# Two graph convolution products of neighbouring batches taken together, with seven products of halves in place of eight

## The chip, the cores and the metric

The kernel runs on one core of a Trainium2 chip. The core has five engines that take their instructions in order, each from a queue of its own: TensorE (PE in the profile; it multiplies matrices and sums into PSUM), VectorE (DVE), ScalarE (ACT), GpSimd (POOL) and SyncE (SP, which here issues nearly all transfers). They meet through semaphores. Matrices lie in SBUF as 128 partitions with so many elements each; larger data lie in DRAM. The metric is the device time of one execution in microseconds (us); lower is better.

## The reference, cut to what matters

`x` has 16 batches of 1024 nodes with 256 channels, `adj` is 1024 x 1024, all float32. Two layers follow each other; the change concerns the second.

```python
# layer 0
c   = mean(x, channels)                                  # one number for each node
A_s = likeness of the nodes by c[m] - c[n]               # 1024 x 1024 for each batch
g   = relu((x^T @ (adj * A_s)) * para)                   # becomes the queries q
k, v = split(x @ kv_w)                                   # 4 heads of 64
x   = layernorm(x + softmax(q k^T * scale) @ v)
# layer 1
h   = relu(x @ w1_loop + adj @ (x @ w1_neigh) + b1)      # 1024 x 128, "first convolution"
h   = relu(h @ w2_loop + adj @ (h @ w2_neigh) + b2)      # 1024 x 256, "second convolution"
x   = layernorm(x + (x + h) * 0.5)
```

The two products concerned are `adj @ t1`, with `t1 = x @ w1_neigh` (1024 x 128), and `adj @ h1`, with `h1` the result of the first convolution (1024 x 128; `w2_neigh` is applied after the product). Both have the same left matrix for every batch, and inner and outer sizes of 1024, 1024 and 128.

## The kernel before, in words

**Staging.** The 16 batches go through a pipeline in which three things share the engines. While the attention of batch b runs, the queries of batch b+1 are formed, and layer 1 of batch b-1 is computed. The order of instructions is written by hand (`run`, from L690, under a manual schedule), so each engine executes its part of the program text in that order. SP issues the transfers in the same order, and a transfer that must wait holds those behind it.

**The attention of a batch.** It has four units (`UNITS`), a pair of heads with half of the query nodes each. `att.scores(u)` (L465 to L486) multiplies keys and queries on TensorE (L473), takes exponentials on ScalarE (L476), sums them on VectorE (L482) and turns the sum (L484). `att.outputs(u)` (L488 to L497) multiplies with the values (L493) and turns the result (L497). `att.add(u)` (L499 to L516) forms the denominators with a small product on TensorE (L505, `den_ps`) and adds the outcome into the residual on VectorE (L509 onwards). Between the units run three functions of `run`:

- `first` (L740): loads x of batch b+1 in blocks; `conv.first` of batch b-1 (L580 to L602): t1 (L585, copied by ScalarE at L588), then for each half of 512 nodes two matmuls with `w1l_sb` (L597) and eight with the adjacency (L599) into the same bank, and the relu on ScalarE (L600). Then `turn_blocks` (L604 to L613): h1 is turned in 32 x 32 blocks on VectorE (L608), stored to DRAM and read back node by node, in two halves. Beside that the moments and the normalization of batch b-2 (`old.moments`, `old.finish`), `prepare` (L202: x of batch b+1 turned to channel-major, and partial sums), `att.add(0)` and `means` (L218).
- `second` (L753): begins the queries of b+1 (`q.left` on GpSimd L387 to L392, `q.likeness`, `q.pair(0)`), then `conv.second` of batch b-1 (`neighbours`, L630 to L637: 2 x 8 matmuls with the adjacency, L635, and copies on ScalarE, L637), then `att.add(1)`.
- `last` (L763): `conv.last` of batch b-1 (L652: `outer` L639 to L643 on TensorE, `residual` L645 to L650 on VectorE), then `att.add(2)`.

After the fourth unit come the other query products (L430), the last `att.add(3)`, the keys (`k_ps`, L307), the values (`v_ps`, L319) and the layer norm of batch b in blocks (`BlockedNorm`, L257 to L297), whose `spread` (L288) writes the result node by node to DRAM and reads it back as `x1`.

**Queries.** `FastQueries` (L367 to L450) already multiplies by halves with seven products in place of eight; its combinations are formed by `left` (GpSimd) and `right` (VectorE).

**Batches at the ends.** In batch 0 the adjacency, read in blocks, is turned on VectorE (`turn_adj`, L718 to L720) into `adjT_sb` (L160), which holds all of it as eight tiles of 128 x 1024 for the rest of the run. Batch 1 is the first with a convolution, that of batch 0. In the last batch there are no queries to form, and the convolution of batch 14 is spread over its end; that of batch 15 follows alone (`conv.first`, `conv.second`, `conv.ending`).

**Buffers.** `row_tile` gives a tile of 128 x 1024 from a ring of `ROWS` = 21 (L69). PSUM has three tiles of 128 x 1024 ("big", two banks of 512 each; `half_psum` takes the first half of one) and two single banks. x has three buffers. The transfer of `x1d` and `h1d` goes through DRAM tiles with two buffers each.

The product of the first convolution is

```python
ph = half_psum(f"h1_ps_{b}_{j}")
for cc in range(NC):
    nc.tensor.matmul(ph, w1l_sb[:, cc, :], xT[:, cc, ts(j, FB)], start=(cc == 0), stop=False)
for mt in range(NT):
    nc.tensor.matmul(ph, t1[:, mt, :], adjT_sb[:, mt, ts(j, FB)], start=False, stop=(mt == NT - 1))
nc.scalar.activation(self.h1T[:, ts(j, FB)], ph, AF.Relu, bias=b1_sb)
```

## Time and profile before

| | |
|---|---|
| time, three runs | 2251.86, 2253.75, 2254.12 us, median 2253.75 |
| the profiled execution | 2252.83 us, its span 2251.1 us, mean granted clock of TensorE 0.998 |
| busy: PE, DVE, ACT, POOL | 99%, 79%, 42%, 8% of the span |
| transfers | 189.39 MB, mean 84 GB/s |
| matmuls h_ps (L599) and u_ps (L635) | 512 records each, 224.9 and 224.5 us busy |
| from the first scores of one batch to those of the next | 138.4 us (the starts are at 154.46, 292.91 and 431.34 for the batches 1, 2 and 3) |

The profile comes from one execution. Its page gives busy time by engine, then the chain of work that ended last, followed back from the end; its shares say which engine's work, or which wait, that chain passes through. A group of instructions has its line, its engine, what it writes and reads, how often it occurs, its busy time and the mean of one in ns, and the idle time of the engine just before it with the engine that ended it ("<-"). In a timeline, each row is one or several adjacent instructions with start and length in us; what stands in brackets is how long the engine had been idle, and who released it. A float32 matmul leaves two records, so 512 records of L599 are 256 matmuls.

## The change

For an adjacency in blocks of 512 x 512, a product of it with one matrix of 1024 x 128 takes four products of blocks, and two matrices (t1 of batch c1 = b-1 and h1 of batch c2 = b-2) take eight. The changed kernel forms both results from seven. t1 and h1, each cut in two halves of 512 nodes, make a 2 x 2 matrix of halves; four sums and differences of them are formed for each pair of batches (`left`), four combinations of the adjacency's blocks once for the whole run (`adj_sums`), and the seven products are put together partly by letting them add up in the same PSUM bank and partly with additions.

- **Adjacency.** `adjT_sb` is gone. Three blocks stay in SBUF (`half_adj` 00, 10 and 11). The fourth (01) and the four combinations (1, 2, 3, 4) are in DRAM; every joint product reads the four combinations into row tiles (`fetch`, 2 x 512 KB each, issued by SP). They are formed in batch 1 by `adj_sums`: eight VectorE subtractions of 128 x 1024, and stores. `turn_adj` turns halves of 512.
- **Joint product.** `Joined.left` is four additions or subtractions on GpSimd (on VectorE in the last joint product). `Joined.run` issues the products 1, 2, 6, 7, 5, 4, 3 with four matmuls of 128 x 512 each, the matmuls with `w1l_sb` (`loop`) ahead of 2 and 3, copies to SBUF on ScalarE, two additions on VectorE and one on GpSimd; at set points between them (`between`) it calls other work. `first` and `third` in it are the two halves of one PSUM tile.
- **Scaling.** `w1l_sb` and `w1n_sb` are multiplied by `LIFT` = 32 at the start, and the relu of the first convolution by 1/32.
- **Pipeline.** The second convolution of a batch now comes one batch later than its first, and its normalization another one later, so that three convolutions are under way (`c1`, `c2`, `c3`). `x1` is read back from DRAM when it is needed (`load_x`) instead of at once; `x1d` has three DRAM buffers.
- **Order.** `gap0` (where `first` was): loads, t1 (`inner`), `att.add(0)`, the fetches 2 and 3, `left`, `prepare`. `means` stands after the second scores. `gap1` (where `second` was): `q.left`, `q.likeness`, the fetches 1 and 4, the joint product, and within it `att.add(1)`, the moments of c3, `q.times_adj`, `q.right(0)` and `finish` of c3. In batch 1, where there is no c2, it runs `c1.first` alone and then `adj_sums`. `gap2`: `last` of c2, `turn_blocks` of c1 with one transpose of 128 x 1024, stores to DRAM (read back at the start of the next batch), `att.add(2)`.
- **Ends.** In the last batch the joint product of batches 14 and 13 runs among the steps of the norm; after it come the joint product of 15 and 14, and the second convolution of 15 alone. `ROWS` is 23.

```diff
-    ROWS = 21
+    ROWS = 23
...
-    adjT_sb = const.tile([P, NT, N], F32, name="adjT_sb")
+    half_adj = {(0, 0): const.tile([P, TJ, FB], F32, name="adjT_00"),
+                (1, 0): const.tile([P, TJ, FB], F32, name="adjT_10"),
+                (1, 1): const.tile([P, TJ, FB], F32, name="adjT_11")}
+    far_adj = {n: dram.tile([2, P, N], F32, tag=f"adj_{n}", name=f"adjT_{n}", bufs=1) for n in ("01", 1, 2, 3, 4)}
...
+    def adj_sums(rows01):
...
+            nc.vector.tensor_sub(v[1], w12, w11)
+            nc.vector.tensor_sub(v[3], w22, w12)
+            nc.vector.tensor_sub(v[2], w22, v[1])
+            nc.vector.tensor_sub(v[4], w21, v[2])
...
-        def turn_blocks(self, j):
+        def turn_blocks(self):
+            h1B = row_tile(f"h1B_{self.b}")
+            nc.vector.transpose(h1B, self.h1T)
...
+    class Joined:
...
+        def left(self, eng):
...
+            eng.tensor_add(s12[:, 0], h1[0], h1[1])
+            eng.tensor_sub(s34[:, 0], t1[0], h1[0])
+            eng.tensor_sub(s12[:, 1], s12[:, 0], t1[0])
+            eng.tensor_sub(s34[:, 1], t1[1], s12[:, 1])
...
+        def run(self, between=None):
...
+            ac = big_psum(f"hu_ps_{b}_0")
+            first, third = ac[:, 0:FB], ac[:, FB:N]
+            second = half_psum(f"hu_ps_{b}_1")
...
+            self.product(1, first, start=True)
+            nc.scalar.copy(p1, first)
+            turn_to(1)
+            c1.loop(third, 0, start=True)
+            self.product(2, third)
+            nc.vector.tensor_add(p1, p1, third)
+            turn_to(2)
+            self.product(6, first, again=True)
+            nc.scalar.copy(u1, first)
+            c1.relu(0, p1)
+            turn_to(6)
+            self.product(7, second, start=True)
+            nc.scalar.copy(p7, second)
+            turn_to(7)
+            self.product(5, first, again=True)
+            nc.scalar.copy(u3, first)
+            turn_to(5)
+            self.product(4, second, again=True)
+            c2.uT = row_tile(f"uT_{c2.b}")
+            nc.vector.tensor_add(c2.uT[:, 0:FB], u1, second)
+            nc.gpsimd.tensor_add(c2.uT[:, FB:N], u3, p7)
+            turn_to(4)
+            c1.loop(first, 1, again=True)
+            self.product(3, first, again=True)
+            c1.relu(1, first)
...
+            def gap0():
                 blocked = load_blocked(b + 1, str(b + 1))
...
+                c1.inner()
+                att.add(0)
+                if both:
+                    c2.load_x()
+                    both.fetch(2, 3)
+                    both.left(nc.gpsimd)
                 ready["xT"], ready["part"] = prepare(blocked, str(b + 1))
...
+                if both:
+                    both.fetch(1, 4)
+                    both.run({1: (lambda: q.left(nc.gpsimd), lambda: q.likeness(0)),
+                              2: (lambda: att.add(1),),
+                              6: (lambda: q.likeness(TJ), c3.moments if c3 else lambda: None),
+                              7: (weigh_first,),
+                              5: (lambda: c3 and c3.finish(out[b - 3]),)})
+                else:
...
+                    c1.first(rows01)
+                    att.add(1)
+                    weigh_first()
+                    store("01", rows01)
+                    adj_sums(rows01)
...
+            def gap2():
+                if both:
+                    c2.last()
+                c1.turn_blocks()
+                att.add(2)
...
+                if u == 1 and between:
+                    ready["mean"] = means(ready["part"], str(b + 1))
```

## What is predicted

> **What bounds the kernel now.** I read the page's busy shares first, then its chain of waits, then one steady batch engine by engine in order of time. The page names the bound:

> ```profile
> PE 2230.0 (99%) x8310; PEld 1067.2 (47%) x8310; DVE 1773.9 (79%) x2377; ACT 945.4 (42%) x1026; POOL 187.6 (8%) x104
> ...
> PE 98%; DVE 1%; DMA 0%; ACT 0%; issue 0%; SPq 0%; POOLq 0%; DVEq 0%; POOL 0%; ACTq 0%
> ```

> TensorE is on the chain for 98% of the span, so instructions taken from it are time gained, and every microsecond that it is newly made to wait is lost. VectorE's 79% is an average and has to be read by stage. In the timeline of TensorE (start, length, then what) the two products of a batch are

> ```profile
> 1004.57 7.03 PE L599 MATMUL h_ps<-adjT_sb,t 128*128 128x512 f32 x16
> 1011.44 1.88 PE L597 MATMUL h_ps<-x1T,w1l_sb 128*128 128x512 f32 x4
> ...
> 1034.79 14.00 PE L635 MATMUL u_ps<-adjT_sb,h 128*128 128x512 f32 x32
> 1048.63 0.30 PE L505 MATMUL den_ps<-den_part,fold 128*128 128x32 f32 x2
> 1048.86 7.14 PE L473 MATMUL s<-qT,kT 64*128 64x512 f32 x32
> ```

> A float32 product leaves two records. From start to start, 8 products of L599 take 6.87 us, 0.859 each; 16 of L635 take 13.84, 0.865 each.

> Where TensorE meets VectorE is at the end of the attention:

> ```profile
> 1070.16 1.23 DVE L647 TENSOR_TENSOR z<-h_ps,b_sb 128x1024 f32<-128x1024 f32 x1 [0.97 <-PE h_ps L643]
> 1071.42 1.23 DVE L650 SCALAR_TENSOR_TENSOR x<-z,x 128x1024 f32<-128x1024 f32 x1
> 1072.56 0.52 DVE L509 RECIPROCAL rden<-den_ps 64x16 f32<-64x16 f32 x2
> ...
> 1089.66 0.71 DVE L497 STREAM_TRANSPOSE o<-av 128x512 f32<-128x512 f32 x1
> ```
> ```profile
> 1089.53 1.02 PE L430 MATMUL g_ps<-T,x 128*128 128x512 f32 x2
> 1090.43 0.41 PE L505 MATMUL den_ps<-den_part,fold 128*128 128x32 f32 x2
> ```

> After the wait of 0.97 VectorE has no gap until the transpose at 1089.66. The fourth denominator (`den_ps`) waits for that transpose, which reads the bank it needs; it starts at 1090.43 instead of 1084.28 + 7 x 0.859 = 1090.29. So TensorE already loses 0.14 us there: from the second half of `last` on, VectorE is as critical as TensorE.

> [...] ScalarE begins 0.20 us after the next product starts (2214.79, then 2214.99), and when that next product must wait for ScalarE it restarts 0.06 after it:

> ```profile
> 2214.99 0.69 ACT L600 ACTIVATE h1T<-h_ps,b_sb 128x512 f32<-128x512 f32 x1 [7.84 <-PE h_ps L599]
> ```
> ```profile
> 2215.74 0.66 PE L620 MATMUL h1n_ps<-ident,h1T 128*128 128x128 f32 x4 [0.34 <-ACT h1T L600]
> ```

> [...]

> **The change part by part.** *Removed.* There are 15 joint products, for batches 1 to 15. Each has 7 x 4 matmuls in place of 8 + 8 of each kind: 16 x 0.859 + 16 x 0.865 - 28 x 0.859 = 3.53 us, 52.9 in all. The h product of batch 0 and the u product of batch 15 stay as they were.

> *Hand-offs inside the joint product.* `first` and `third` are halves of one PSUM tile. In the changed kernel's instructions the first `loop` matmul (into `third`) waits for ScalarE's copy of `first`, and product 6 (into `first`) for VectorE's addition of `third`. All of TensorE's queue stands behind each. Copy: 0.20 + 0.59 (the L637 row) + 0.06 = 0.85, and I take 0.88 for the 0.06 to 0.14 of restart. Addition: 0.20 + 0.69 (L441) + 0.06 = 0.95 less the denominator of about 0.2 that lies between = 0.75. The other copies lie beside a whole product (3.44 us) and cost nothing; product 5 and 4 wait for copies finished 2 us before.

> *`turn_blocks` moved.* Two 512-wide transposes (0.71) left a stage where VectorE idled; one of 1024 (1.25, as L484) now stands between L650 and L509 above. Nothing before the transpose `o` can absorb it, as z waits for TensorE: the denominator is late by 1.25 more. `att.add(1)`, the moments and `finish` move into the joint product, where VectorE is to be free by some 58 us into the batch and the scores start at 62: nothing.

> *The mean.* It now stands behind the second scores. Counted from the batch's first scores, `den_ps` 0 comes at 17.8; VectorE's `add(0)` (2.9, as from 1048.97) ends at 20.95 and `prepare` (4.45, as from 1013.00) at 25.4. TensorE is there at 25.1 to 25.2: 0.3. The blocks of x must have landed by 22; before they landed at 24.1, behind two loads of 1 MB, of which one is now behind them and 0.5 MB takes its place: about 21.5. Bounds 0 and 2.

> *POOL.* Four more operations of 1.265 (the L389 row) run at 19 to 23, beside the two two-input operations of `add(0)`. Between 0 (VectorE goes first) and 1.3 (it waits once), and the delayed accumulation may push the addition of `third` by up to 1 more. I take 0.2.

> *DMA.* Four matrices of 1 MB per joint product, 63 MB on 187. The SP queue issues fetches 2 and 3 behind the blocks of x, 1 and 4 behind `q.load`: landing by about 34 and 46, needed at 42 and 49. Hidden inside batches. Row tiles: 8 more in use with 2 more and others freed early; their waits in the instruction list fall on work done before. POOL's scaling of weights and the stores: hidden by 100 us of attention.

> *Batch 1, where no second convolution exists.* TensorE has 20.8 us less there (moved to the end), but VectorE gets 8 subtractions of 1024 (1.22, L268), 9.8 us, in front of the third accumulation. In the batch's time: h product 33 to 50, `add(1)` to 53, weights to 58, sums to 68, accumulation and part 11.7 to 79.8. TensorE is through `av` at 64.4, and its next instruction, the third denominator, waits: 15.4. [...] I take 17.2; both ends 12 (if the sums wait for nothing and the clock holds) and 20.

> *The two joint products at the end.* The copy of t1 is not hidden: 0.20 + 1.01 (L588) + 0.06 = 1.27 each. Hand-offs about 1.4 each, as denominator and folds lie inside them. In the last one, fetch 2 is issued behind the output of batch 12, itself behind `finish`: eight 512 KB loads at 1.75 to 2.2 us, first wanted some 3.5 us before it lands. 3 to 7, I take 4. Together 9.4.

> *The adjacency turned in halves.* Four transposes of 1024 took 4.61 us (L720, from 123.77); eight of 512, 0.64 apart, take 5.1, ahead of the weighting (L349) for which TensorE waited 1.14 us: 0.5 once.

> *Sum* against the profile's own span: 2251.1 - 52.9 + 13 x (0.88 + 0.75 + 1.25 + 0.3 + 0.2 = 3.38) + 17.2 + 9.4 + 0.5 = 2269.2, that is +18.1. The median of the three other runs is 2253.75, 2.65 above that span (the time of the profiled execution itself is 2252.83): 2271.9.

> **Rivals.** *VectorE keeps pace.* Then `den_ps`, the mean and batch 1 don't wait: 13 x 1.75 + 17.2 = 40 less, 2231. For it: VectorE loses `add(1)` from the stretch before the third accumulation, and it is 79% busy overall. Against it: that accumulation starts when the exponentials allow, not when VectorE is free (1052.01 after scores at 1048.86), and the 0.14 above. It decides if VectorE's waits come to under 22 us of these 40: then the kernel isn't slower.

> *The whole saving arrives*: 2253.75 - 52.9 = 2201, if the hand-offs are hidden too. Both waits are in the instruction list, so this is unlikely.

> [...] and about 0.7 more at the addition or the landing of x: 26 more, 2297. For it: four POOL operations beside two-input work in each batch. Against: DMA has room, 38.6% busy on q1.

> *It does not do what it says.* The instruction list has 28 matmuls and 4 of `loop` in each joint product; I leave this at nothing.

> **How the numbers follow.** Forecast 0.58, VectorE keeps pace 0.18, whole saving 0.04, [...] 0.20. Unknown costs alone make the forecast 2255 to 2285 (mean 0 to 2 over 13 batches is the widest, taken by half; batch 1 from -5 to +3; the last fetch -1 to +3). Range 2240 to 2297: it leaves out the faster half of the second case and the third. No change means within 0.2%, 4.5 us, about what a measurement of this kernel can tell. Slower: 0.52 of the forecast and 0.20, so 0.73 with 0.01 of the second; same 0.09, the forecast's low end and the second's high end; faster 0.18.

> **What would show it.** In the profile after: 60 x 2 fewer records of the two products and TensorE's busy share well under 99%; idle before `loop` of about 0.7 to 0.9 a time, at product 6 0.7, at `den_ps` about 1.3 a batch on the transpose `o`; one idle of 12 to 17 us in the second batch; batches of 138.3 instead of 138.45 us (scores at 154.46 and 292.91). Wrong if batches take under 136.5, or if the second batch has no such idle.

## The result and the profile after

The changed kernel takes 2291.32 us (median of 4 runs, 2289.91 to 2295.66) against 2253.34 before: a ratio of 1.0173, 95% interval 1.0155 to 1.019. That is 38.0 us slower, where 18.1 were forecast. The sign was right and the range holds the time, but the change is 2.1 times as large as forecast.

The page of the changed kernel, its busy shares and the chain that ended last:

```profile
PE 2201.1 (96%) x8190; PEld 1046.9 (46%) x8190; DVE 1852.9 (81%) x2413; ACT 964.4 (42%) x1056; POOL 326.0 (14%) x177
...
PE 69%; DVE 17%; SPq 4%; issue 4%; ACT 3%; DMA 3%; POOL 0%; DVEq 0%; POOLq 0%; ACTq 0%
```

TensorE has the 120 records less that were foreseen (8310, now 8190), and it now waits: 96% busy instead of 99%, and the chain leaves it for VectorE in 17% of the span. What it waits for is in the view of its waits (line and tile that waited, who ended it: us in total, times, longest):

```profile
PE mean_ps L256 <- DVE part L249: 14.7, 26, 1.0
PE den_ps L545 <- DVE o L537: 14.6, 13, 1.1
PE hu_ps L769 <- issue: 10.4, 14, 0.8
PE hu_ps L636 <- ACT snap L786: 10.0, 15, 0.7
PE den_ps L545 <- DVE den_part L526: 6.1, 1, 6.1
PE s L513 <- ACT pr L516: 5.7, 2, 3.8
...
PE hu_ps L769 <- DMA adj<-adjT: 3.3, 1, 3.3
PE hu_ps L769 <- ACT t L632: 2.2, 2, 1.1
```

Rows two to four are the fourth denominator, product 6 and the `loop` matmul, each where the prediction put it. The first row, the mean, is the largest and was forecast as one of the smallest. Rows five and six are batch 1, the last two the ending. In a steady batch (one of the 13 from batch 2 to batch 14) TensorE's timeline shows them one after the other:

```profile
726.60 7.14 PE L513 MATMUL s<-qT,kT 64*128 64x512 f32 x32
733.98 0.41 PE L256 MATMUL mean_ps<-part,fold 128*128 128x32 f32 x2 [0.24 <-DVE part L249]
735.11 0.41 PE L256 MATMUL mean_ps<-part,fold 128*128 128x32 f32 x2 [0.72 <-DVE part L249]
735.45 7.09 PE L533 MATMUL av<-pr,v 128*64 128x512 f32 x32
742.47 3.70 PE L769 MATMUL hu_ps<-adjT,t 128*128 128x512 f32 x8
746.84 1.98 PE L636 MATMUL hu_ps<-x1T,w1l_sb 128*128 128x512 f32 x4 [0.68 <-ACT snap L786]
...
752.10 0.30 PE L545 MATMUL den_ps<-den_part,fold 128*128 128x32 f32 x2
753.16 10.54 PE L769 MATMUL hu_ps<-adj,R 128*128 128x512 f32 x24 [0.76 <-issue]
...
812.88 1.02 PE L470 MATMUL g_ps<-T,x 128*128 128x512 f32 x2
815.03 0.41 PE L545 MATMUL den_ps<-den_part,fold 128*128 128x32 f32 x2 [1.13 <-DVE o L537]
```

The number in brackets is only the idle time that the records leave: the first record behind a wait starts that much after the end of the one before it. The price of a wait is better read from start to start, less the pitch of 0.859 for a matmul: 746.84 - 742.47 - 4 x 0.859 = 0.93 for the copy; 753.16 - 752.10 less 0.2 for the denominator = 0.86 for the addition; 815.03 - 812.88 - 0.86 = 1.29 for the fourth denominator; and 1.33 for the mean (735.45 - 726.60 less the 7.06 that the scores take, which is 1.79, less some 0.46 that its four thin matmuls took before, where nothing waited). The label "issue" at product 6 is no cause: VectorE's addition ends at 753.06, 0.10 before it.

Where the 37.0 us between the two profiled spans (2251.1 and 2288.1) lie is seen from the first scores of each batch:

| stretch | before | after | difference | forecast |
|---|---|---|---|---|
| up to batch 1 | 154.46 | 154.83 | +0.4 | +0.5 |
| batch 1 | 138.45 | 135.18 | -3.3 | -3.6 (+17.2, less 20.8 moved to the end) |
| each steady batch (2 to 14) | 138.44 | 139.53 | +1.09 | -0.15 |
| 13 of them | | | +14.2 | -2 |
| more in the late ones among them | | 0.2, 0.7, 2.2, 0.7 | +3.8 | 0 |
| from batch 15 on | 158.4 | 180.3 | +21.9 | +23.1 (20.8 - 7.1 + 9.4) |

Batch 1 and the ending came out within 1.3 us. The 13 steady batches were to gain 2 and lost 18.

## Experiments

Each experiment edits the changed kernel, and the gains are told against its 2291.32 us. The kernel before, run again beside each group of experiments, took 2252.5 to 2253.5 us, so a difference between groups is good to about 1 us.

The first question is why the mean is late. VectorE's timeline in the same batch, with the like instruction of batch 1, where `left` does not run, as first line:

```profile
174.41 0.69 DVE L555 TENSOR_TENSOR xB_a<-xB_a,o 128x512 f32<-128x512 f32 x1
...
727.47 0.68 DVE L553 TENSOR_TENSOR o<-o,rden 128x512 f32<-128x512 f32 x1
728.19 1.64 DVE L555 TENSOR_TENSOR xB_a<-xB_a,o 128x512 f32<-128x512 f32 x1
729.86 0.69 DVE L556 TENSOR_REDUCE sums<-xB_a 128x16 f32<-128x512 f32 x1
730.47 2.36 DVE L216 STREAM_TRANSPOSE xT<-xB 128x1024 f32<-128x1024 f32 x2
732.75 2.30 DVE L249 TENSOR_REDUCE part<-xB 128x32 f32<-128x1024 f32 x2
```

And GpSimd's:

```profile
727.65 1.63 POOL L760 TENSOR_TENSOR R<-t,h 128x512 f32<-128x512 f32 x1 [2.19 <-ACT t L632]
729.24 1.73 POOL L761 TENSOR_TENSOR R<-R,t 128x512 f32<-128x512 f32 x1
731.04 1.28 POOL L762 TENSOR_TENSOR R<-t,R 128x512 f32<-128x512 f32 x1
```

The addition in `att.add(0)` (L555) takes 1.64 instead of 0.69. Of its 64 instances in the run exactly 13 are long, one in each steady batch. The trace shows a chain of operations with two inputs on the two engines. L760 on GpSimd ends 1.13 us after VectorE's multiplication L553 (at 728.15), VectorE's L555 ends 0.55 after L760 (at 729.28), and L761 ends 1.14 after L555 (at 729.83). Each needs after the other's end what it takes alone (1.27, 0.69 and 1.27), less 0.13 to 0.14, as if it had waited for that end. Beside VectorE's operations with one input nothing of the kind is seen in these lines: L556 takes its 0.69 beside L761, and L762 its 1.28 beside the transposes. What makes the two wait for each other is not shown. Against this reading of the late mean stands another: the mean is late because x comes late behind larger transfers.

### The meeting with `left`, or the transfers

`left` without three of its operations:

```diff
-            eng.tensor_sub(s34[:, 0], t1[0], h1[0])
-            eng.tensor_sub(s12[:, 1], s12[:, 0], t1[0])
-            eng.tensor_sub(s34[:, 1], t1[1], s12[:, 1])
-            self.x = {1: t1[0], 2: t1[1], 3: s34[:, 1], 4: h1[1], 5: s12[:, 0], 6: s12[:, 1], 7: s34[:, 0]}
+            self.x = {1: t1[0], 2: t1[1], 3: s12[:, 0], 4: h1[1], 5: s12[:, 0], 6: s12[:, 0], 7: s12[:, 0]}
```

> Of the four operations of left on GpSimd only the first is issued; the products 3, 6 and 7 read its result in place of theirs, so this leaves out three of the four combinations (the number and size of the matmuls stay). Theory A[...]: in the changed kernel the second operation of left (1.63 us) and the two-input addition of add(0) on VectorE (L555, 1.64 instead of 0.69 us) exclude each other, and everything behind it on VectorE, the mean included, is late by 0.95. Without these operations L555 is back at 0.69, the two waits of mean_ps fall from 0.96 to about 0.1 to 0.3 us in a steady batch, and the kernel gains about 0.9 x 10 to 0.95 x 13, that is 9 to 12 us: about 2280. Theory B, the transfers: the mean is late because the blocks of x land late behind and beside the fetched matrices; then L555 may be short, but the transposes of x wait for a DMA instead, and the time stays within 2 us of 2291.

Measured: 2323.49 us (2319.31 to 2334.49), 32 slower. The run decides for both theories in part. L555 takes 0.69 in all 64 instances, as theory A says. But the mean's wait falls only from 14.7 to 6.9, some 0.5 a batch where A expected 0.1 to 0.3, and the transposes of x now wait for their transfer, as theory B says. VectorE's waits for it, in the changed kernel and then here:

```profile
DVE xT L216 <- DMA xB<-in_x_dram: 1.6, 3, 0.6
```
```profile
DVE xT L216 <- DMA xB<-in_x_dram: 5.1, 9, 0.9
```

The late addition had hidden most of a late landing. The time got longer, against both theories, because a far larger wait came up. TensorE's waits, then ScalarE's and VectorE's timeline in one batch, and the like instruction of the changed kernel (the numbers of lines behind `left` are smaller by 3 in this run):

```profile
PE hu_ps L636 <- ACT snap L783: 35.5, 15, 2.6
```
```profile
754.69 0.59 ACT L783 COPY snap<-hu_ps 128x512 f32<-128x512 f32 x1 [12.38 <-DVE accB L524]
```
```profile
742.82 10.50 DVE L522 TENSOR_TENSOR acc<-acc,pr 128x1024 f32<-128x1024 f32 x6
```
```profile
736.29 9.63 DVE L522 TENSOR_TENSOR acc<-acc,pr 128x1024 f32<-128x1024 f32 x6
```

GpSimd runs the four operations of `q.left` in one piece into VectorE's second accumulation, which takes 10.50 for six additions (9.63 in the changed kernel with two of the four beside it, 7.87 without company). And ScalarE's copy of `first` waits for the transpose `accB` to end; in the changed kernel it starts at 746.21, while `accB` runs until 747.21. Probably it gets another row tile of the ring, which is not shown. So the `loop` matmul waits up to 2.6 instead of 0.7, and in 8 of the 13 steady batches the clock falls to half for 3.4 us behind this wait (the granted clock of the whole run was 0.988, in the changed kernel 0.994). Taking work away moved the rest of GpSimd's queue to a worse place: the run shows that the collision makes L555 long, and it does not show its price in time.

The second try leaves nothing out. It shifts `left` to a time at which VectorE has one-input work:

```diff
-            if c2 and more:
-                c2.load_h1()
             def gap0():
                 blocked = load_blocked(b + 1, str(b + 1))
+                if both:
+                    c2.load_h1()
```

> The load of h1 (512 KB) is issued behind the blocks of x of the next batch instead of ahead of them; nothing is left out. The blocks land about 1.5 us earlier, and h1, which left waits for, about 7 us later, so that left runs beside one-input work (transposes and reductions of x). Theory A[...]: L555 takes 0.69 us in every batch, mean_ps waits 0 to 0.3, and also the four batches that took 0.2 to 2.2 us more than the others fall in line: 13 x 0.95 + 3.8 = 16 us less, about 2275. Theory B (transfers alone): only the batches in which a transpose of x waits for a DMA gain, at most 4 us: 2287.

Measured: 2277.96 us (2276.43 to 2278.89), 13.4 less. L555 is at 0.69 in all 64 instances; in the batch read, the first three operations of `left` take 1.27 to 1.28 beside the transposes and reductions of x. The mean waits 0.3 us once in the whole run, and a steady batch takes 138.57, 0.96 less. Theory B allowed 4 us. But this edit moves both: in the traces the last block of x lands at 19.7 to 22.1 us into the batch instead of 21.5 to 23.6. With the run before it, in which the transfers are issued as in the changed kernel, the two causes can be told apart: GpSimd's operations make L555 long, and with L555 short the landing of x still keeps about half of the mean's wait (6.9 of 14.7).

### The hand-offs inside the joint product

```diff
-            ac = big_psum(f"hu_ps_{b}_0")
-            first, third = ac[:, 0:FB], ac[:, FB:N]
-            second = half_psum(f"hu_ps_{b}_1")
+            third, second, first = (half_psum(f"hu_ps_{b}_{n}") for n in "321")
```

> first, second and third of the joint product each get a PSUM tile of their own, third allocated first; nothing else changes. Theory: the waits of the loop matmul for the copy of first (0.93 us a batch, start to start against the pitch of a matmul) and of product 6 for the addition of third (0.86) exist only because first and third are halves of one tile. Both vanish: 13 x 1.79 + 2 x 1.2 = 26 us less, about 2265. Rival: VectorE is as late as TensorE there, and the denominator of unit 1 or the scores of unit 2 take the wait over; then at most half of it arrives, 2278 or more.

Measured: 2266.45 us (2264.68 to 2273.56), 24.9 less; 137.67 for a steady batch, 1.86 less. Both waits are gone from the list. No data passes between the copy of `first` and the matmul into `third`, so it was the common PSUM tile that made one wait for the other; VectorE did not take the wait over.

### turn_blocks at another place

```diff
                     adj_sums(rows01)
+                c1.turn_blocks()
             def gap2():
                 if both:
                     c2.last()
-                c1.turn_blocks()
                 att.add(2)
```

> turn_blocks moved from behind the residual (gap2) to the end of gap1, where VectorE is idle for 6 us until the first exponentials of unit 2; nothing else changes. Theory: the transpose of 1.25 us is what makes the fourth denominator wait for the transpose o (1.29 us a batch). Back to the 0.03 to 0.14 of before: 13 x 1.2 = 15 to 16 us less, about 2276. Rival: VectorE's work in that stage is late anyway (the residual waits for TensorE, the second reciprocal stands behind it), and the denominator's wait stays at 0.5 or more: 2284 or more.

Measured: 2278.82 us (2276.92 to 2279.25), 12.5 less; 138.46 for a steady batch, 1.07 less, and the fourth denominator's wait falls from 14.6 to 0.4 in the whole run. The same transpose costs 1.07 behind the residual and nothing 23 us earlier.

### The mean at another place

```diff
-                if u == 1 and between:
-                    ready["mean"] = means(ready["part"], str(b + 1))
...
             def gap1():
+                ready["mean"] = means(ready["part"], str(b + 1))
```

> The matmuls of the mean and what follows on VectorE stand behind the outputs of unit 1 instead of ahead of them; nothing is left out. Theory: the mean's wait[...] costs TensorE 1.24 us a batch and a further 3.8 in four batches; behind the outputs nothing waits for it, as the row of means is only wanted by ScalarE at 41 us into the batch. 13 x 1.24 + 3.8 = 20 us less, about 2271. Rival: the row of means, now behind the transpose of the outputs on VectorE (0.7 us later), delays the first weights and with them the copies of the joint product on ScalarE; then new waits of about 0.7 a batch take its place and 9 us or fewer arrive.

Measured: 2277.97 us (2276.34 to 2278.09), 13.4 less, between the two expectations. The mean's wait is gone; the shortest steady batches take 138.35, 1.18 less, and 8 of the 13 are within 0.1 us of that. But a new wait took its place, half as large as the rival said and in another place: VectorE's addition of `third` is late, not ScalarE's copies. VectorE's and TensorE's timeline:

```profile
747.33 0.71 DVE L267 TENSOR_TENSOR own<-mean,quarter 128x32 f32<-128x32 f32 x1
748.07 0.19 DVE L270 TENSOR_REDUCE c_col<-own 128x8 f32<-128x32 f32 x1
748.18 0.68 DVE L790 TENSOR_TENSOR snap<-snap,hu_ps 128x512 f32<-128x512 f32 x1
```
```profile
748.95 10.54 PE L769 MATMUL hu_ps<-adj,R 128*128 128x512 f32 x24 [1.13 <-POOL S L432]
```

The addition starts as soon as the means' last step is through, and product 6 idles 1.13 instead of 0.76; the releaser that is named, GpSimd's `S`, is not read by it. It is the wait that the own tiles remove. The late batches did not vanish either: one of them takes 141.68, with 2.4 us of idle at this same product and 3.4 us at half the clock behind it (24 matmul records that take 10.54 in the batch above take 12.24 there, and the granted clock from 1720 to 1740 was 0.91).

### Batch 1

```diff
                     c1.first(rows01)
-                    att.add(1)
-                    weigh_first()
                     store("01", rows01)
                     adj_sums(rows01)
+                    att.add(1)
+                    weigh_first()
```

> In batch 1 the eight subtractions of adj_sums are issued ahead of add(1), where VectorE was idle for 11.1 us waiting for the denominator; nothing is left out. Theory: the stall of batch 1 (6.1 us at the third denominator, 5.7 at the scores, and some 4 of matmuls at half the clock) vanishes: 15 to 17 us less, about 2275. Rival: the row tiles that the sums hold until their stores have landed delay the exponentials of unit 2 all the same (5.7 us and the clock stay), and half or less arrives: 2284 or more.

Measured: 2284.07 us (2280.86 to 2288.58), 7.3 less. Neither side was right. The scores' wait of 5.7 vanished, so with this order the stores do not hold the exponentials. But the third denominator still waits 5.5 for `den_part`. VectorE now runs the first weights (5 us) where the subtractions were, in front of the third accumulation. The second attempt moves those too (the edit is shown against the first attempt):

```diff
-                    adj_sums(rows01)
-                    att.add(1)
-                    weigh_first()
+                    adj_sums(rows01, 0)
+                    weigh_first()
+                    att.add(1)
...
                 kT = keys(b + 1, xT, norm.variance)
+                if not c2:
+                    adj_sums(rows01, 1)
                 norm.scale()
```

> Batch 1 again, by VectorE's whole order: ahead of add(1) stand half of the subtractions (4) and the first weights; the other four stand where VectorE waits for the power on GpSimd (5.6 us, before the norm's scale), and in this batch alone turn_blocks stands behind add(2); nothing is left out. With all eight ahead of add(1) the scores' wait of 5.7 us vanished, but the third denominator still waited 5.5, since the first weights (5 us of VectorE) stood in front of the third accumulation. Theory: it is VectorE's order alone; now the accumulation starts with the second exponential, the denominator waits less than 1, the clock holds, and batch 1 takes about 118 to 119 us instead of 135.2: 2275. Rival: the row tiles or their stores hold the exponentials; a wait of 3 or more stays in batch 1: 2281 or more.

Measured: 2280.15 us (2277.59 to 2285.37), 11.2 less. In batch 1 the theory holds: the denominator waits 0.8, and the batch takes 120.2 instead of 135.2. Some of it is given back in other batches of the profiled execution (144.4 and 142.3 in two of them): x lands at 24.6 and 23.9 us into these batches, and the mean waits for it. In the first of them, behind waits of 1.94 and 0.72, 26 matmul records of the outputs take 8.74 us, where 32 take 7.09 in the changed kernel's batch shown above.

### The ending

The first edit puts t1 of batch 14 ahead of the last outputs, t1 of batch 15 and its fetches ahead of `last` of batch 13:

```diff
+                if u == 3 and not more:
+                    c1.inner()
                 att.outputs(u)
...
                 c1.turn(0)
+                convs[b] = GraphConv(b, norm.x1T, norm.nodes)
+                final = Joined(convs[b], c1)
+                final.fetch(2, 3, 1, 4)
+                convs[b].inner()
                 c2.last()
                 c1.turn(1)
                 c3.moments()
                 c3.finish(out[b - 3])
```

> Ending alone: t1 of batch 14 is formed ahead of the outputs of the last unit, t1 of batch 15 and the four fetches of the last joint product are issued ahead of the second convolution's end of batch 13 and of the output of batch 12; nothing is left out. Theory: the two waits for the copy of t1 (1.10 each) and the wait for the fetched matrix (3.34) vanish: 5 to 6 us less, about 2286. Rival: the fetches contend with the loads of x1 and their row tiles come free late; the wait stays at 2 or more: 2288 to 2291.

Measured: 2291.74 us (2284.69 to 2296.58), no gain. The waits for t1 and the fetch are gone and another stands in their place:

```profile
PE hu_ps L769 <- DVE snap L790: 4.6, 1, 4.6
```

VectorE reaches the addition of `third` only after the moments and the normalization of batch 12. So the order on VectorE was put right too (again shown against the first attempt):

```diff
                 c1.turn(1)
-                c3.moments()
-                c3.finish(out[b - 3])
+                final.left(nc.vector)
...
+        final.run({2: (c4.moments, lambda: c4.finish(out[B - 4]), c1.load_x),
                    4: (lambda: c1.turn(0), c3.moments, lambda: c3.finish(out[B - 3]))})
```

> The ending again: as in the first attempt, but with left ahead of the moments and output of batch 12, which move behind the addition of third. The first attempt removed the waits for t1 and for the fetch and got one of 4.6 us for VectorE's addition of third, behind moments and finish on its queue. Theory: with VectorE's order put right the 1.10 + 1.10 + 3.34 us arrive: 5 to 6 less, about 2286. Rival: the four fetches, x1 and the outputs contend there, and product 6 or 7 waits 2 or more for a transfer: 2288 or more.

Measured: 2286.04 us (2282.33 to 2288.32), 5.3 less; from batch 15 on it takes 173.9 instead of 180.3.

### Together

The five edits (own tiles, `turn_blocks`, the mean, batch 1 and the ending; not the later load of h1), with the first versions for batch 1 and the ending:

> All five edits together: own PSUM tiles, turn_blocks at the end of gap1, the mean behind the outputs, adj_sums ahead of add(1), the ending's order. Theory: the terms are separate waits of TensorE and add up: 26 + 16 + 20 + 16 + 5 = 83 us less than the changed kernel, about 2208, that is 45 less than the kernel before. Rival: with TensorE faster, VectorE (81% busy) becomes the bound of a batch and at least a third of the gain is lost: 2235 or more.

Measured: 2219.51 us (2219.25 to 2220.22), a ratio to before of 0.9851 (0.9837 to 0.9864). A steady batch takes 135.28; the three single differences give 139.53 - 1.86 - 1.07 - 1.18 = 135.42, so they add up and VectorE does not become the bound. What is missing lies in batch 1 (6.6 us at the denominator) and in the ending (4.3). With the second versions:

> Own PSUM tiles, turn_blocks at the end of gap1, the mean behind the outputs, and the two new orders for batch 1 and the ending. Theory: the terms add up, as VectorE's idle time takes what is moved. From 2219.5 (all five of the first attempt) batch 1 gains 8 to 9 (6.6 us of wait and the clock behind it) and the ending 4 to 5: about 2206, that is 47 less than the kernel before, of the 52.9 that the removed matmuls are worth. Rival: VectorE takes the place again in one of the two, and 2213 or more is measured.

Measured: 2206.85 us (2205.71 to 2209.84), a ratio of 0.9798 (0.9785 to 0.9811): 46 us faster than the kernel before, of the 52.9 that the removed matmuls are worth. The page, and TensorE's waits in the whole run (the numbers of lines from 200 on are smaller by one in this run; the waits for x and for `wg` lie in batch 0, as in the kernels above):

```profile
PE 2180.5 (99%) x8190; PEld 1041.6 (47%) x8190; DVE 1861.7 (84%) x2413; ACT 964.0 (44%) x1056; POOL 329.9 (15%) x177
```
```profile
PE xT_ps L226 <- DMA x<-in_x_dram: 4.9, 2, 4.7
PE den_ps L544 <- DVE o L536: 2.4, 2, 1.4
PE g_ps L396 <- DVE wg L388: 1.8, 1, 1.8
PE den_ps L544 <- DVE den_part L525: 0.8, 1, 0.8
PE s L512 <- ACT qT L403: 0.7, 1, 0.7
```

The last run adds the shifted load of h1, with which, in the run above, the addition in `att.add(0)` did not meet `left` (0.69 in all 64 instances):

> The last kernel, and the load of h1 behind the blocks of x[...]. Theory: the meeting still happens in the last kernel, but since nothing of TensorE waits for the mean any more it costs nothing: the same time within 2 us. Rival: VectorE's 0.95 us a batch count somewhere else (the addition of third, the denominator of unit 1): 4 to 12 us less.

Measured: 2209.09 us (2208.57 to 2212.86), 2.2 more, just outside the 2 us, and no gain. In the kernel without the shift the addition in `att.add(0)` is still long 13 times (GpSimd is busy 329.9 us there, 326.0 in the changed kernel), and its steady batches take 135.28 all the same. So the collision cost time only where TensorE waited for what stands behind it.

## Why the prediction came out as it did

**Right.** TensorE's saving, and that it does not arrive because it is now made to wait. The copy was put at 0.88 and measured 0.93, the addition at 0.75 and 0.86; taking both away gave 1.86 against a sum of 1.63. The transpose of `turn_blocks` was put at 1.25; the wait is 1.29, and moving it gave 1.07. Batch 1 was put at +17.2 and came to about +17.5, the ending at +9.4 and came to about 8. The idle times named as signs are there. Two signs are not: batches take 139.5 instead of 138.3, and batch 1 has no single idle of 12 to 17 us, which the prediction itself had called a sign of being wrong.

**The step that failed: "Between 0 (VectorE goes first) and 1.3 (it waits once) ... I take 0.2."** The place had been named, with the right pair of operations, but of bounds that were the author's estimate (from the 1.265 us of one GpSimd operation) the low end was taken. VectorE waits in every steady batch, by 0.95. The order is not a matter of chance from batch to batch: GpSimd's second operation is released by ScalarE's copy of t1 and starts at 727.65, VectorE's addition comes at 728.19, and the products on which the two hang, t1 and the denominators behind it, stand next to each other in TensorE's queue. To choose between the two bounds, these two times were needed. With the mean (taken as 0.3) the place was put at 0.5 and measured 1.33: 0.83 x 13 = 10.8 of the 37.0 - 18.1 = 18.9 us that the sum is short. This meeting is not all of it. A landing of x at "about 21.5" was the other thing that the small number rested on.

**"Hidden inside batches."** The transfers were said to land in time, x by about 21.5 where 22 was wanted. In the trace the last block of x lands at 21.45 to 23.59, in the batch shown at 22.09. Behind the delayed addition the second transpose starts at 23.02, so this is soon enough in most batches; with a short addition it would start at 22.07 and wait, as the run without three of the operations showed. Meeting and landing overlap: with the long addition the late landing is mostly hidden, and with the short one it keeps about half of the mean's wait. In three batches x lands so late that a transpose waits 0.4 to 0.6 us even behind the long addition. This lateness, and in one batch the clock (0.50 granted for 3.4 us), make 3.8 more. Hand-offs larger by 0.16 a batch are 2.1; some 0.25 a batch, 3.2, is what is left of the difference, and I can't place it. Batch 1, the ending and the start together take 1.1 back: 10.8 + 3.8 + 2.1 + 3.2 - 1.1 = 18.8.

**Batch 1 was right in sum and wrong in its parts.** That the waits of the row tiles "fall on work done before" does not hold there. The exponentials of unit 2 waited for row tiles: 3.91 and 0.70 us for VectorE's subtractions to be through with one, 0.51 and 0.38 for the store of a combination. So 5.7 us of TensorE's wait came ahead of the denominator and 6.1 at it. The rest, by subtraction, is put down to two stretches of 6.8 us at half the clock (0.50 granted from 215.02 and from 232.08 on). The prediction's step from 15.4 to 17.2 was an estimate of the author's that no trace of the kernel before shows.

**The rivals.** The third one (2297, with 0.20) was nearest in time, and right that both of its causes act: 0.95 a batch where GpSimd's operations meet VectorE's addition, which it had put at 1.3, and a landing of x that would have been late without it. "VectorE keeps pace" would have asked for another place of the mean and of `turn_blocks`: with these two, own tiles and the new orders of batch 1 and the ending it does, at 84% busy.

## What to carry to other kernels

An engine that is 79% busy can take on more only where it is idle: cost a moved or added instruction against the gaps of that engine at that place, and against what stands behind it in the queue, then look for a gap nearby, since the same transpose cost 1.07 us a batch in one place and nothing 23 us earlier. Where operations of two engines may have to wait for each other, as VectorE's addition did here (1.64 us for 0.69), work out from the trace when each of the two instructions becomes ready; here the collision came in all 13 steady batches, and once TensorE no longer waited for what stands behind it, avoiding the collision brought nothing. When two causes delay the same instruction, taking one away shows only what the other leaves (here 6.9 of 14.7 us), so look in the trace for the wait that the first one hid. Before giving up a change that removes work and comes out slower, undo its new waits one by one: here the change was worth 46 us once nothing new stood in TensorE's way.

## What the runs showed of the hardware that was not expected

The clock fell after short waits of TensorE. In one steady batch of the changed kernel the waits of the mean, 0.78 and 0.72 us with two thin matmuls between them, were followed by outputs that took 8.67 us instead of 7.09. TensorE's timeline, and the stretch's row (length, busy time and instructions of PE, PEld, DVE, ACT and POOL, granted clock, share and rate of the transfers):

```profile
1712.13 0.41 PE L256 MATMUL mean_ps<-part,fold 128*128 128x32 f32 x2 [0.78 <-DVE part L249]
1713.26 0.47 PE L256 MATMUL mean_ps<-part,fold 128*128 128x32 f32 x2 [0.72 <-DVE part L249]
1713.66 8.67 PE L533 MATMUL av<-pr,v 128*64 128x512 f32 x32
```
```profile
1713.00:1717.00 4.00, 3.74 (x10) 1.35 (x12) 3.79 (x4) 0.00 (x0) 0.00 (x0) 0.57 1.03 411
```

Also not expected: a run with less work was 32 us slower. What was left on GpSimd's queue moved up into VectorE's accumulation, ScalarE's copy came late behind it, and the clock fell behind TensorE's longer waits (2.6 us at the longest; 0.988 granted over the run).
